# A scratch write on GpSimd between the gathers of a graph convolution

## The chip, the core and the metric

The kernel runs on one core of one Trainium2 chip. The time is in device microseconds (us). PE is the matrix engine, DVE the vector engine, ACT the scalar engine, POOL is GpSimd, and SP is the engine that issues most plain transfers. "L614" is line 614 of the kernel before.

## The reference, cut to what matters

A graph has N = 6250 nodes with D = 128 features and E = 200000 edges, sorted by destination. After a layer norm and a ReLU, two convolutions and one attention layer follow.

```
def mesh_conv(x, src, dst, ea, w1, b1, g, bt, w2, b2):
    m = concatenate([x[dst], x[src], ea]) @ w1 + b1        # one row for each edge
    m = silu(group_norm(m, g, bt)) @ w2 + b2
    return segment_sum(m, dst) / clip(count(dst), 1)       # mean over a node's edges

h = mesh_conv(h, ...); h = silu(group_norm(h)) + t_emb_term
h = mesh_conv(h, ...); h = silu(group_norm(h)) + h0
o = softmax attention over each node's edges, projected, normed
out = x + h + o
```

The change lies in the two convolutions alone.

## The kernel before, in words

For each convolution a node stage first multiplies all nodes by the two halves of `w1`. The half for destinations goes to DRAM as three bf16 pieces (`a3_d`), the half for sources as fp32 (`b_d`, 512 bytes a node). Then the edges run through in 196 chunks of CH = 1024 edges (NT = 8 groups of 128).

For one chunk, `ahead` does four things. `loads` fetches over SP's queue the relative destinations (`rel_b`), the edge attributes (`ohT`) and a window of destination rows (`pk`); DVE makes a one-hot matrix of `rel_b` (L454). `gather` issues eight indirect DMAs on POOL (L459), each fetching 128 source rows of `b_d` into the chunk's buffer `g`. `hidden` lets PE multiply the one-hot matrix by the window (L578, 24 products of 128x128) into PSUM `m`.

`first` adds `m` to the gathered rows (L590, DVE), squares them (L592, ACT) and sums them for the variances (L593). After a run of up to eight chunks `deviations` makes the factors, and `second` finishes one chunk: three DVE passes over `g` (L604, L607, L608), silu (L609, ACT), a one-hot matrix of destinations (L465), the product that sums the edges of a node (L614, PE, into `u`), two masked copies (L648, ACT) and an addition into the table (L639, DVE).

`pipeline` writes this order out: at step n `ahead(n+1)`, then `first(n)`, then `second` of a chunk some eight older. There are G + 5 = 13 buffers `g`, used in turn, so the gathers of chunk c must wait for L614 of chunk c-13.

The order in which each engine's instructions stand in the program is settled when it is built: instructions of one engine are placed by a scheduler that looks at their dependencies and at when it expects the engine to be free, not by the order of the Python lines alone. Each engine then works through its own list in that order. Behind the 196 chunks stands a loop for edges that fit no window (`leftovers`), which all engines enter and leave together. After the second convolution comes attention, with gathers of `kv_d`.

Of the kernel before, what the change touches and what calls it, by code (L numbers as in the profile page):

```python
# [8 lines left out]
FP = mybir.dt.float32  # L9
# [10 lines left out]
P = 128  # L20
# [2 lines left out]
HD = 16  # L23
NT = 8
CH = NT * P
G = 8
WN = 112
KE = P - WN
# [9 lines left out]
def kernel(ctx: ExitStack, tc: tile.TileContext, x, src, dst, eat, w, out):  # L38
# [10 lines left out]
    nc = tc.nc  # L49
# [392 lines left out]
    def loads(c, pools, rows_d):  # L442
        k = Chunk()
        k.c = c
        k.src, k.dm = src_i[:, c * NT:(c + 1) * NT], dm0[:, c * NT:(c + 1) * NT]
        k.rel = pools["rel"].tile([WN, CH], BF, name="rel_b")
        nc.sync.dma_start(
            out=k.rel, in_=rel_d[c * NT:(c + 1) * NT, :].rearrange("t p -> (t p)")[None, :].to_broadcast([WN, CH]))
        k.ohT = pools["ohT"].tile([P, CH], BF, name="ohT")
        nc.sync.dma_start(out=k.ohT[WN:P, :], in_=ea_d[:, c * CH:(c + 1) * CH])  # L450
        k.pk = pk[c % NPK]
        first = value(lo_i, c, SP, N - 1)
        nc.sync.dma_start(out=k.pk[:WN].rearrange("p s c -> p (s c)"), in_=rows_d[bass.ds(first, WN), :])
        nc.vector.tensor_scalar(k.ohT[:WN, :], k.rel, iota_p[:WN], None, ALU.is_equal)  # L454
        return k

    def gather(k, g, table_d):
        for t in range(NT):
            nc.gpsimd.indirect_dma_start(  # L459
                out=g[:, t, :table_d.shape[1]], out_offset=None, in_=table_d,  # L460
                in_offset=bass.IndirectOffsetOnAxis(ap=k.src[:, t:t + 1], axis=0))
# [7 lines left out]
    def leftovers(body, pools):  # L469
# [5 lines left out]
        with tc.For_i(0, nout, 1) as c:  # L475
# [3 lines left out]
            with tc.For_i(0, n, 1) as r:  # L479
# [13 lines left out]
                k.win = nc.s_assert_within(at + r, 0, NW - 1, skip_runtime_bounds_check_because=WHY)  # L493
                k.ea = lp.tile([KE, CH], BF, name="l_ea")
                nc.sync.dma_start(out=k.ea, in_=ea_d[:, bass.ds(c * CH, CH)])
                body(k)
# [17 lines left out]
    def spread(n):  # L514

        sizes = [G] * max(0, (n - 5) // G)
        rest = n - sum(sizes)
        while rest:
            s = min(max(rest // 2, 1), G)
            sizes.append(s)  # L520
# [26 lines left out]
    def conv(i):  # L547
# [4 lines left out]
        with ExitStack() as es:  # L552
# [3 lines left out]
            gp, wk, vp = pool("gp", 1), pool("wk", 2), pool("vp", 2)  # L556
            ps_ = pools["ps"]

            gs = [gp.tile([P, NT, PITCH], FP, name=f"g{j}") for j in range(G + 5)]
            if i == 1:  # L560
# [11 lines left out]
            def hidden(k, terms):  # L572
                k.m = ps_.tile([P, NT, D], FP, name="m", tag="m", bufs=2)
                for t in range(NT):
                    e = slice(t * P, (t + 1) * P)
                    pairs = [(lhs[:, e], rhs[:, s, :]) for lhs, rhs in terms for s in range(3)]
                    for j, (a, b) in enumerate(pairs):
                        nc.tensor.matmul(k.m[:, t, :], lhsT=a, rhs=b, start=(j == 0), stop=(j == len(pairs) - 1))  # L578

            def ahead(c):  # L580
                k = loads(c, pools, a3_d[i])
                k.g = gs[c % len(gs)]
                gather(k, k.g, b_d[i])
                hidden(k, [(k.ohT, k.pk)])
                return k

            def first(k, var, j):

                k.mt = k.g[:, :, :D]
                nc.vector.tensor_tensor(k.mt, k.m, k.mt, ALU.add)  # L590
                sq = wk.tile([P, NT, D], FP, name="sq")
                nc.scalar.activation(sq, k.mt, AF.Square)  # L592
                return lambda: nc.vector.tensor_reduce(  # L593
                    var[:, j * NT * H:(j + 1) * NT * H], sq.rearrange("p t (g c) -> p (t g) c", c=HD), AX.X, ALU.add)

            def deviations(n, var):
                sd = vp.tile([P, G * NT * H], FP, name="sd")
                nc.scalar.activation(sd[:, :n], var[:, :n], AF.Sqrt, bias=eps_t, scale=1.0 / HD)
                rs = ps_.tile([P, G * NT * H], FP, name="rs")
                nc.vector.reciprocal(rs[:, :n], sd[:, :n])  # L600
                return rs
# [17 lines left out]
            def first_step(k):  # L619
                for f in state["reduce"]:  # L620
                    f()
                if state["j"] == 0:
                    state["var"] = vp.tile([P, G * NT * H], FP, name="var")
                state["reduce"] = [first(k, state["var"], state["j"])]
# [17 lines left out]
            def second(k):  # L642
# [7 lines left out]
                state["late"].append(k)  # L650

            pipeline(ahead, first_step, between, second, add_late)

            wcl = pools["left"].tile([KE, 3, D], BF, name="wcl")
# [17 lines left out]
    def after_conv(i, A):  # L672
# [15 lines left out]
        nc.scalar.activation(A[:, :NW, :], A[:, :NW, :], AF.Silu)  # L688

    conv(1)  # L690
    with tc.tile_pool(name="node1", bufs=1) as np_:
        A = np_.tile([P, NW + 1, D], FP, name="A")
        after_conv(1, A)
        nc.vector.tensor_tensor(A[:, :NW, :], A[:, :NW, :], temb[:, None, :].to_broadcast([P, NW, D]), ALU.add)
        make_ab(A, 2)
    conv(2)
    with tc.tile_pool(name="node2", bufs=1) as np_:
        A = np_.tile([P, NW + 1, D], FP, name="A")
# [25 lines left out]
    with ExitStack() as es:  # L724
# [3 lines left out]
        gp, wk = pool("gp", G + 3), pool("wk", 2)  # L728
# [271 lines left out]
```

## Time and profile before

| | |
|---|---|
| median of 3 runs | 8192.53 us (8170.84 to 8251.86) |
| profiled execution | 8242.21 us, span 8240.4 us |
| mean granted PE clock | 0.666 |
| POOL busy | 4542.3 us (55%), 4723 instructions |
| DVE busy | 5153.9 us (63%) |
| PE busy | 3684.0 us (45%) |
| ACT busy | 1631.0 us (20%) |
| gathers of the convolutions (L459) | 3136 of 949 ns |
| first gather of the first, second convolution | 213.17 us, 2888.77 us |

Busy time is the sum of an engine's rows. A row of the timeline gives start, duration, engine, line, operation, what it writes and reads, how often, and in brackets how long the engine had been idle and what ended that. A row of the waits gives who waited for whom, the sum in us, the number of times and the longest. A row of the windows gives a stretch, its length, then busy time and number of instructions of PE, the weight loads, DVE, ACT and POOL, then the clock, the share of time in which the DMA engines were busy and GB/s. "remote" stands for a wait whose releaser the profile does not show, "issue" for time in which the engine waited for nothing that it shows.

### The profile page before, as it was taken

Reading aid. Unit: us, or ns where it says so; the run is one execution under the profiler, and the core shown is the slowest. Engines: PE = TensorE matmul, PEld = TensorE weight load, DVE = VectorE, ACT = ScalarE, POOL = GpSimd, SP = SyncE. Lnnn points to the kernel's source line nnn. Section 1 sums busy time; section 2 is a strip of 40 time slices with the busy share of each in tenths; the row PEclk is TensorE's granted clock in tenths of the full one; section 3 lists DMA queues with packets and bytes.
Section 4 is the critical chain, followed back from the end, with each engine's and each line's share of the span. In section 5 each row is a group of like instructions: output and inputs, shape, how many; then the busy total and the mean of one; then the engine's idle time right before and its main releaser. Section 6 shows DMA issues by size and latency. Waiting matters only on the chain. (4 is left out here: it accounts for less than half of the span.)

```text
span 8240.4 us, 87011 instructions
## 1 busy us (share of the span) xinstructions
PE 3684.0 (45%) x26465; PEld 3255.2 (40%) x26466; DVE 5153.9 (63%) x7719; ACT 1631.0 (20%) x3110; POOL 4542.3 (55%) x4723
## 2 busy tenths in 40 slices
PE   2144444444444414444444444442555555555553
PEld 1133343334334313433334433332444545544542
DVE  5266666666666726666666666683666666666666
ACT  2122222222222312222222222230000000000001
POOL 2556566666565056656656665504666666666650
PEclk9566666666666656666666666676676666666666
DMA  5222222222222122222222222213444444444441
GB/s 160 63 70 71 69 74 73 71 72 73 68 70 65 43 61 73 70 68 72 72 70 71 73 73 69 65 71 111 118 120 120 120 120 120 120 120 118 120 110 48
DMA packets 422049, 702.81 MB, mean 85 GB/s; under 512 B 116780, under 2 KB 237444, under 8 KB 421060
## 3 DMA queue, kind: packets, MB, share of 16 engines
q0 software_dynamic: 175616, 417.77, 18.7%
q1 hardware_dynamic: 210920, 258.43, 10.3%
q10 hardware_dynamic: 35036, 20.95, 0.9%
q8 instruction: 215, 3.52, 0.2%
q14 instruction: 262, 2.15, 0.1%
HBM read 649.99 MB, written 46.67 MB: 85 GB/s over the span
## 5 line engine op out<-in xcount | busy, mean ns | idle before, releaser
L459 POOL DMA_INDIRECT g<-b_d,src_i x3136 | 2977.0, 949 | 2227.8 <-PE u L614 785.5
L459 POOL DMA_INDIRECT g<-kv_d,src_i x1568 | 1523.4, 972 | 1164.6 <-issue 418.7
L614 PE MATMUL u<-g,oh 128*128 128x129 f32 (+1 forms) x6272 | 1292.0, 380 | 1309.6 <-ACT g L609 659.9
L614 PEld LDWEIGHTS u<-g,oh 128*128 128x128 f32 x6272 | 1183.8, 286 | 1418.7 <-ACT g L609 710.8
L578 PE MATMUL m<-pk,ohT 128*128 128x128 bf16 x9408 | 894.5, 258 | 1609.9 <-issue 977.8
L578 PEld LDWEIGHTS <-ohT 128*128 128x128 bf16 x9408 | 744.8, 118 | 1742.4 <-issue 1170.7
L639 DVE TENSOR_TENSOR flat<-flat,u 128x258 f32 (+1 forms) x392 | 164.2, 419 | 1343.2 <-ACT u L648 1178.1
L828 PE MATMUL u<-g,oh 128*128 128x145 f32 x3136 | 785.8, 438 | 420.6 <-issue 361.7
L828 PEld LDWEIGHTS u<-g,oh 128*128 128x128 f32 x3136 | 723.7, 318 | 454.8 <-issue 391.0
L648 ACT ACTIVATE u<-u,mask 128x129 f32<-128x129 f32 (+1 forms) x784 | 266.5, 340 | 2152.5 <-remote 1250.7
L590 DVE TENSOR_TENSOR g<-m,g 128x1024 f32<-128x1024 f32 x392 | 476.2, 1215 | 290.8 <-remote 232.8
L740 PE MATMUL qe<-pk,ohT 128*128 128x128 bf16 x4704 | 439.1, 257 | 367.0 <-DVE g L752 226.3
L609 ACT ACTIVATE g<-g 128x1024 f32<-128x1024 f32 x392 | 414.1, 1056 | 925.8 <-DVE g L608 471.4
L592 ACT ACTIVATE sq<-g 128x1024 f32<-128x1024 f32 x392 | 414.3, 1057 | 718.6 <-DVE g L590 438.7
L740 PEld LDWEIGHTS <-ohT 128*128 128x128 bf16 x4704 | 382.4, 119 | 406.1 <-issue 204.2
L872 DVE SCALAR_TENSOR_TENSOR nm<-u,nm 128x2 f32<-128x2 f32 x196 | 31.2, 159 | 768.1 <-remote 467.6
L454 DVE TENSOR_SCALAR ohT<-rel_b,iota_p 112x1024 bf16<-112x1024 bf16 x588 | 299.1, 514 | 331.6 <-remote 313.4
L593 DVE TENSOR_REDUCE var<-sq 128x64 f32<-128x1024 f32 x392 | 473.8, 1209 | 15.5 <-ACT sq L592 13.7
L465 DVE TENSOR_TENSOR oh<-cps,dm 128x1024 f32<-128x1024 f32 x392 | 476.7, 1216 | 0.0
L607 DVE TENSOR_TENSOR g<-g,cps 128x1024 f32<-128x1024 f32 x392 | 475.1, 1212 | 1.8
L608 DVE TENSOR_TENSOR g<-g,cps 128x1024 f32<-128x1024 f32 x392 | 475.2, 1212 | 0.2
L604 DVE TENSOR_TENSOR g<-g,rs 128x1024 f32<-128x1024 f32 x392 | 473.8, 1209 | 0.1
(196 smaller groups left out, 3563.9 us busy)
## 6 DMA issues: line engine op xcount, KB each, us to landing
rel_b<-rel_d SPq DMA_DIRECT2D x588, 224.0 KB
g<-b_d,src_i POOLq DMA_INDIRECT x3136
pk<-a_d SPq DMA_DIRECT2D x588, 84.0 KB
g<-kv_d,src_i POOLq DMA_INDIRECT x1568
ohT<-ea_d SPq DMA_DIRECT2D x588, 32.0 KB
a_d<-a SPq DMA_DIRECT2D x48, 192.0 KB
kv_d<-kv ACTq DMA_DIRECT2D x49, 132.0 KB
h_d<-A SPq DMA_DIRECT2D x2, 3136.0 KB
```

Of the source, the lines that this page charges most:

```text
L459: nc.gpsimd.indirect_dma_start(out=g[:, t, :table_d.shape[1]], out_offset=None, in_=table_d, in_offset=bass.IndirectOffsetOnAxis(ap=k.src[ ...
L465: nc.vector.tensor_tensor(k.oh, iota[:, None, :].to_broadcast([P, NT, P]), k.dm[:, :, None].to_broadcast([P, NT, P]), ALU.is_equal)
L578: nc.tensor.matmul(k.m[:, t, :], lhsT=a, rhs=b, start=(j == 0), stop=(j == len(pairs) - 1))
L590: nc.vector.tensor_tensor(k.mt, k.m, k.mt, ALU.add)
L592: nc.scalar.activation(sq, k.mt, AF.Square)
L593: return lambda: nc.vector.tensor_reduce(var[:, j * NT * H:(j + 1) * NT * H], sq.rearrange("p t (g c) -> p (t g) c", c=HD), AX.X, ALU.add)
L604: nc.vector.tensor_tensor(k.mt.rearrange("p t (g c) -> p t g c", c=HD), k.mt.rearrange("p t (g c) -> p t g c", c=HD), k.rs.rearrange("p (t ...
L607: nc.vector.tensor_tensor(k.mt, k.mt, over_edges(gam), ALU.mult)
L608: nc.vector.tensor_tensor(k.mt, k.mt, over_edges(bet), ALU.add)
L614: nc.tensor.matmul(k.u[:, 0, :wide], lhsT=k.oh[:, t, :], rhs=k.g[:, t, :wide], start=(t == 0), stop=(t == NT - 1))
L740: nc.tensor.matmul(qe[:, t, :], lhsT=lhs[:, e], rhs=rhs[:, s, :], start=(s == 0), stop=(s == 2))
L828: nc.tensor.matmul(k.u[:, :wide], lhsT=k.oh[:, t, :], rhs=k.g[:, t, :wide], start=(t == 0), stop=(t == NT - 1))
```

## The change

A constant REST = 1280 is added. In each convolution a scratch tile `rest` of 128 x 1280 fp32 is taken from the pool `wk` with one buffer, and `ahead` writes zeros to it with a memset on GpSimd, in the Python code behind the eight gathers of the chunk. Nothing reads the tile.

```
+REST = 1280
...
+            rest = wk.tile([P, REST], FP, name="rest", bufs=1)
+
             def ahead(c):
                 k = loads(c, pools, a3_d[i])
                 k.g = gs[c % len(gs)]
                 gather(k, k.g, b_d[i])
+                nc.gpsimd.memset(rest, 0.0)
                 hidden(k, [(k.ohT, k.pk)])
                 return k
```

The chunks of `leftovers` and the attention layer do not use it. There are 2 x 196 = 392 such memsets. In the changed program they differ from each other in no way that the scheduler would see: each writes the same tile, waits for the memset before it, and is awaited by no other engine.

More of the change, by code (lines that the diff above doesn't have):

```diff
@@ L25 @@
 CH = NT * P
+REST = 1280
 G = 8
@@ L578, in hidden @@
                         nc.tensor.matmul(k.m[:, t, :], lhsT=a, rhs=b, start=(j == 0), stop=(j == len(pairs) - 1))
+            rest = wk.tile([P, REST], FP, name="rest", bufs=1)
             def ahead(c):
@@ L583, in ahead @@
                 gather(k, k.g, b_d[i])
+                nc.gpsimd.memset(rest, 0.0)
                 hidden(k, [(k.ohT, k.pk)])
```

## The prediction

> **What bounds the kernel now.** I read the page first (engines, costliest groups), then POOL's waits, then windows over single stretches, then the timeline where stages meet. The trace is of one core at a mean granted clock of 0.666.
>
> ```profile
> PE 3684.0 (45%) x26465; PEld 3255.2 (40%) x26466; DVE 5153.9 (63%) x7719; ACT 1631.0 (20%) x3110; POOL 4542.3 (55%) x4723
> ...
> L459 POOL DMA_INDIRECT g<-b_d,src_i x3136 | 2977.0, 949 | 2227.8 <-PE u L614 785.5
> ```
>
> No engine is full. POOL's row understates it: a gather shows as 949 ns, but on the timeline the next one starts 1.25 us after the last. A chunk's eight gathers so cost POOL 10.0 us, and the 392 chunks of the convolutions follow each other at 12.56 us (the additions of L590, chunk 20 to chunk 188 of the first convolution: 2110 us over 168). POOL is 80% taken in the loops and has 2.5 us to spare per chunk.
>
> ```profile
> ACT u L648 <- remote: 1250.7, 137, 22.7
> ...
> POOL g L459 <- PE u L614: 785.5, 288, 55.1
> ```
>
> POOL's spare time is waiting for a free gather buffer: chunk c takes the buffer of chunk c-13, free when its L614 product is done. So compute sets the pace. What holds compute is in the other line: ACT waits 1250.7 us in L648 for a mark that no row explains. One case:
>
> ```profile
> 2031.08 2.02 PE L614 MATMUL u<-g,oh 128*128 128x129 f32 x16 [2.37 <-issue]
> ...
> 2036.22 0.95 POOL L459 DMA_INDIRECT g<-b_d,src_i  x1 [0.30 <-issue]
> ...
> 2039.15 0.94 POOL L459 DMA_INDIRECT g<-b_d,src_i  x1 [1.98 <-remote]
> 2039.21 0.72 ACT L648 ACTIVATE u<-u,mask 128x129 f32<-128x129 f32 x2 [8.28 <-remote]
> ```
>
> PE's product ends at 2033.1 by its row; ACT, which needs it, starts at 2039.21, about when POOL's train of gathers pauses for 1.98 us. This repeats along the loop: while gathers run back to back, PE's completions reach the others late. Keep this for the third rival.
>
> How far the gathers run ahead of use decides what a later gather costs:
>
> ```profile
> 837.62 0.94 POOL L459 DMA_INDIRECT g<-b_d,src_i  x1 [0.59 <-remote]
> ...
> 871.55 1.21 DVE L590 TENSOR_TENSOR g<-m,g 128x1024 f32<-128x1024 f32 x1
> ...
> 3309.99 0.94 POOL L459 DMA_INDIRECT g<-b_d,src_i  x1 [0.30 <-issue]
> ...
> 3342.43 1.21 DVE L590 TENSOR_TENSOR g<-m,g 128x1024 f32<-128x1024 f32 x1
> ```
>
> The first pair is chunk 48 of the first convolution (last gather, then its first use), the second is chunk 32 of the second: 33.0 and 31.5 us from the end of gathering to use. Chunk 0's data came 1.6 us after its last gather (223.23 to 224.87), so the slack is 31.4 and 29.9 us.
>
> **What the Trainium skill says.** "GPSIMD Engine Reference", section "Engine selection", puts one-input work on GpSimd at about line rate; with the clock and width of its section "Specifications" (1.2 GHz, eight cores of 16 fp32) 1280 columns are an estimated 1.07 us. "Perfetto Trace Analysis", section "GPSIMD Engine Instruction", says to time such instructions by start-to-start spacing, not by their rows; the gathers agree (1.25 against 0.949 us). "SBUF — State Buffer", section "Who interferes with whom", says a VectorE instruction with two SBUF inputs contends only with a GpSimd one that reads SBUF. The scratch write reads nothing, so I charge DVE nothing; no line of this trace shows it.
>
> **The change part by part.** It adds 392 memsets of 128x1280 fp32 on POOL and nothing else; apart from a few neighbours exchanged on DVE, ACT and SP, costed at nothing, the other engines keep their order. But the memset depends only on the memset before it, and the built order does not put one behind each chunk. First convolution: 70 ahead of the first gather, 1 ahead of chunk 13, 125 in groups (mostly 3 or 4, every eighth chunk 10 or 11) from chunk 15 to ahead of chunk 48, none later. Second: 129 ahead of the first gather, 2 ahead of chunk 13, 65 up to ahead of chunk 32. So it is four lumps, not a rest per chunk.
>
> Price of one:
>
> ```profile
> 0.28 0.10 POOL L986 MEMSET const-float32-0.0<- 128x1 f32 x1
> ...
> 0.76 0.20 POOL masks.py:197 MEMSET ident<- 128x128 f32 x1 [0.29 <-POOLq L986]
> ```
>
> One column takes 100 ns and 128 take 205 (groups view), 0.83 ns per column: 1.16 us for 1280. Each memset also waits on POOL's own mark of the one before; POOL wakes 0.08 us after ACT's marks (a cast ends at 108.94, ea_f starts at 109.02). I take 1.25 us; the bounds are 1.16 (wait free) and 1.5 (the 0.30 us that lies between gathers).
>
> Lump 1. The first memset waits for the last ea_b cast and its store (issued at 129.90), so it starts near 132; 70 x 1.25 = 87.5 ends at 220. The cover is POOL's 84.83 us of idle time:
>
> ```profile
> 213.17 1.30 POOL L459 DMA_INDIRECT g<-b_d,src_i  x1 [84.83 <-DVE g L562]
> ...
> 2740.86 0.20 DVE L676 TENSOR_SCALAR icnt<-flat 128x49 f32<-128x49 f32 x1 [2.31 <-issue]
> ...
> 2888.77 0.94 POOL L459 DMA_INDIRECT g<-b_d,src_i  x1 [238.78 <-SPq L435]
> ```
>
> It runs out 7 us too early, and chunk 0's use follows its gather by 1.6 us, so all 7 us count.
>
> Lump 3. The 129 stand behind the loop that closes the first convolution, which all engines leave together; DVE's first instruction after it is at 2740.86. 129 x 1.25 = 161 ends at 2902, 13 us behind the old first gather. (The 238.78 us of idle time are no cover as a whole: 90 of them lie before the loop's end.)
>
> Lumps 2 and 4, in the loops:
>
> ```profile
> 393.00:839.00 446.00, 190.88 (x1415) 167.75 (x1413) 279.50 (x286) 110.09 (x154) 273.84 (x288) 0.67 0.24 69
> 3073.00:3311.00 238.00, 111.75 (x792) 97.65 (x792) 157.35 (x160) 60.59 (x85) 151.75 (x160) 0.66 0.25 71
> ```
>
> These windows are chunks 13 to 48 and 13 to 32; the last bracket before the clock counts the gathers. 288 x 1.25 = 360 of 446 us: 86 spare. The lump is 125 x 1.25 = 156, so chunk 48's data come 70 us later; 31 are slack, 39 reach DVE at L590. In the second 160 x 1.25 = 200 of 238: 38 spare, 81 added, 43 late, 30 slack, 13 reach DVE. Behind the waiting L590 stand, in DVE's order, the second pass of older chunks and with it the release of the buffers.
>
> After each lump the lead is gone and must be rebuilt by gathers back to back, the situation of the 2039 case. Its harsh form is the start: in the 131 us of chunks 0 to 12 only three L590 finish before the train ends at 343. Rebuilding three chunks of lead should cost less; bounds 0 (it rebuilds in waits that exist anyway) and 33 us (compute stands still meanwhile). I take 16 each.
>
> Sum: 7 + 39 + 13 + 13 + 2 x 16 = 104 us. On the profiled execution (8242.2, span 8240.4) that gives 8346; that run lies 0.6% above the median of the three timed ones, 8192.5, and on their scale it is about 8297.
>
> **The rivals.**
> - Mostly hidden: the lumps lie in waits, memsets cost 1.16 us, rebuilding is free. Lumps 1 and 3 then give 0 and 2, the loops 28 and 7: about 37, or less where a relieved PE gives some back. For it: 785.5 us of buffer waits. Against: the spare per stretch is counted above. Time 8220.
> - Dearer memset, 1.5 us: lumps 24, 70, 46 and 30, with rebuilding 202; time 8395. For it: the 0.30 us between gathers. Against: the bare memsets at the start follow each other in 0.03 us.
> - Faster: the pauses let PE's marks through. Place: L648, 1250.7 us over 392 chunks, 3.2 us each; over the 55 chunks of lumps 2 and 4 at most 176. But POOL's own work in chunks 13 to 48 must fit 446 + 31 us for the gain to arrive, so it decides only if a memset costs POOL under about (477 - 360) / 125 = 0.94 us, and for most of the gain under 0.7. A half to two thirds of the 176 gives 8085. Against: both memset rows and the skill's rate.
> - A rest behind every chunk, as the diff reads, would lie in each chunk's 2.5 us and relieve all 392. The built order rules it out.
>
> **How the numbers follow.** Forecast 0.55 (own range 8240 to 8350), hidden 0.20, dearer 0.15, faster 0.10. A measurement tells about 1% (82 us) from no change. Of the forecast some three quarters lie over 1%: 0.42, with the dear case 0.57 slower. Hidden, the rest of the forecast and a little of the faster case make 0.35 within 1%; 0.08 faster. The range of 8200 to 8400 leaves out the faster case and the dear one's upper half.
>
> **What would show it.** Right: 392 memset rows near 1.16 us, none after about 900 us in the first convolution; the first gathers near 220 and 2910; between chunks 30 and 48 ACT's L592 or DVE's L590 waiting for gathers; POOL's waits for PE u L614 smaller. Wrong: memsets starting under 1.0 us or over 1.5 us apart, L590 of chunk 48 no later than 871 plus lump 1's shift, or L648's wait for remote falling by hundreds of microseconds with no gather late.

## The result, and the profile after

The changed kernel takes 8293.42 us (median of 9 runs, 8281.94 to 8308.44); the kernel before, run beside it, 8191.32 us (9 runs, 8151.82 to 8251.86). The ratio is 1.0138, with a 95% interval from 1.0117 to 1.0158: 96 to 129 us more. The forecast was 8297 us, 104 us more. In the kernel after, the lines around the change stand one to four lower: L459 is L460, L590 is L594, L592 is L596, L614 is L618, L648 is L652; the memset is L587.

The page of the kernel after, first the engines, then the costliest groups (busy us, mean ns, idle time before and what ended it), with the group of the memsets:

```profile
PE 3679.1 (44%) x26465; PEld 3273.2 (39%) x26466; DVE 5169.5 (62%) x7719; ACT 1631.3 (20%) x3110; POOL 4998.1 (60%) x5115
...
L460 POOL DMA_INDIRECT g<-b_d,src_i x3136 | 2971.2, 947 | 1730.0 <-issue 742.0
...
L594 DVE TENSOR_TENSOR g<-m,g 128x1024 f32<-128x1024 f32 x392 | 476.3, 1215 | 506.1 <-DMA g<-b_d,src_i 259.3
...
L587 POOL MEMSET rest<- 128x1280 f32 x392 | 463.5, 1182 | 109.8 <-DVEq L476 85.9
```

POOL has 392 more instructions and 456 us more of busy time; the other engines execute as many instructions as before. What is new is in the third line: the additions now wait 259.3 us for gathers. In the kernel before, the waits view has 14.6 us for that pair.

The memsets also slow some of DVE's work. The addition L594 takes 1215 ns in both kernels, but DVE's busy time is 15.6 us higher, and 10.4 of them are in the one-hot matrix L454. Its source view in the kernel before, after, and in the one with memsets of double length that comes below (durations min/median/max in ns):

```profile
L454 DVE TENSOR_SCALAR ohT<-rel_b,iota_p x588: 468/480/714, 190.9 to 8071.8; 112x1024 bf16<-112x1024 bf16 x196
```

```profile
L455 DVE TENSOR_SCALAR ohT<-rel_b,iota_p x588: 467/481/1460, 190.4 to 8118.4; 112x1024 bf16<-112x1024 bf16 x196
```

```profile
L455 DVE TENSOR_SCALAR ohT<-rel_b,iota_p x588: 466/481/2549, 191.5 to 8299.2; 112x1024 bf16<-112x1024 bf16 x196
```

In the changed kernel the 23 of these rows that overlap a memset take 0.95 us on average, the other 565 take 0.51 and none of them over 0.73. That is 10 us of DVE's time in all. Whether any of it reaches the end of the kernel, no run separates.

The lead of a chunk is the time from the end of its gathers to the start of its use, the addition. The timeline of the kernel after, at the places that the prediction named (start, duration, engine, line, operation; in brackets the idle time before it):

```profile
131.26 3.61 POOL L587 MEMSET rest<- 128x1280 f32 x3 [4.12 <-DMA ea_d<-ea_b]
...
220.77 1.30 POOL L460 DMA_INDIRECT g<-b_d,src_i  x1 [0.19 <-DMA ohT<-ea_d]
...
907.89 0.94 POOL L460 DMA_INDIRECT g<-b_d,src_i  x1 [0.30 <-remote]
...
910.49 1.22 DVE L594 TENSOR_TENSOR g<-m,g 128x1024 f32<-128x1024 f32 x1 [6.25 <-DMA g<-b_d,src_i]
...
2801.21 1.17 POOL L587 MEMSET rest<- 128x1280 f32 x1 [85.95 <-DVEq L476]
...
2959.75 0.95 POOL L460 DMA_INDIRECT g<-b_d,src_i  x1 [0.15 <-issue]
...
3412.95 0.94 POOL L460 DMA_INDIRECT g<-b_d,src_i  x1 [0.30 <-DMA g<-b_d,src_i]
...
3415.65 1.22 DVE L594 TENSOR_TENSOR g<-m,g 128x1024 f32<-128x1024 f32 x1 [6.32 <-DMA g<-b_d,src_i]
```

The fourth line is the use of chunk 48 of the first convolution, the last that of chunk 32 of the second; the gather above each is that chunk's last. Before, 33.0 and 31.5 us lay between the end of that gather and its use. Now 1.7 and 1.8 us do (908.84 to 910.49, 3413.89 to 3415.65), and the addition names the gather as what it waited for: the lead is gone. Chunk 48's use has moved from 871.55 to 910.49, by 38.9 us. Seven chunks on, when the lead is back at 31 us, the shift is 55.4 us.

A warning about the two profiles: from one to the other the spans differ by 48 us only, against 102 us between the medians. The attention stage, which the change doesn't touch, is 24 us shorter in the trace after. Over all the traces of this study, its length is either 2785 to 2798 us or 2815 to 2822, for kernels whose source is the same there. The profiled execution of the kernel before lies 51 us above the median of its runs beside it. Nor is a convolution free of it: in the kernel below that has memsets in the second convolution alone, the unchanged first one is 37.9 us longer than before, and its chunk 20 is used 10.3 us later. A lead is read within one trace and is firm. A shift of 10 or 20 us between two traces is firm only where several pairs of traces show it, and a total of a few tens of microseconds isn't.

### The profile page after: what moved, and what is told of

Its sections match the earlier page's. It is cut to its first block, busy times and chain, and to the rows that moved or that the text cites. A ratio compares the mean times of both kernels' runs of the same rounds, so it can differ in the third digit from the quotient of the medians.

```text
span 8288.4 us, 87405 instructions
## 1 busy us (share of the span) xinstructions
PE 3679.1 (44%) x26465; PEld 3273.2 (39%) x26466; DVE 5169.5 (62%) x7719; ACT 1631.3 (20%) x3110; POOL 4998.1 (60%) x5115
## 5 line engine op out<-in xcount | busy, mean ns | idle before, releaser
L460 POOL DMA_INDIRECT g<-b_d,src_i x3136 | 2971.2, 947 | 1730.0 <-issue 742.0
L460 POOL DMA_INDIRECT g<-kv_d,src_i x1568 | 1520.9, 970 | 1144.3 <-issue 417.9
L618 PE MATMUL u<-g,oh 128*128 128x129 f32 (+1 forms) x6272 | 1299.4, 384 | 1234.9 <-ACT g L613 792.3
L618 PEld LDWEIGHTS u<-g,oh 128*128 128x128 f32 x6272 | 1196.0, 290 | 1348.3 <-ACT g L613 867.2
L594 DVE TENSOR_TENSOR g<-m,g 128x1024 f32<-128x1024 f32 x392 | 476.3, 1215 | 506.1 <-DMA g<-b_d,src_i 259.3
L652 ACT ACTIVATE u<-u,mask 128x129 f32<-128x129 f32 (+1 forms) x784 | 266.5, 340 | 1997.3 <-remote 1209.4
L596 ACT ACTIVATE sq<-g 128x1024 f32<-128x1024 f32 x392 | 414.2, 1057 | 920.7 <-DVE g L594 527.5
L587 POOL MEMSET rest<- 128x1280 f32 x392 | 463.5, 1182 | 109.8 <-DVEq L476 85.9
L466 DVE TENSOR_TENSOR oh<-cps,dm 128x1024 f32<-128x1024 f32 x392 | 476.3, 1215 | 0.0
```

What stands on the lines that cost most here:

```text
L460: nc.gpsimd.indirect_dma_start(out=g[:, t, :table_d.shape[1]], out_offset=None, in_=table_d, in_offset=bass.IndirectOffsetOnAxis(ap=k.src[ ...
L466: nc.vector.tensor_tensor(k.oh, iota[:, None, :].to_broadcast([P, NT, P]), k.dm[:, :, None].to_broadcast([P, NT, P]), ALU.is_equal)
L587: nc.gpsimd.memset(rest, 0.0)
L618: nc.tensor.matmul(k.u[:, 0, :wide], lhsT=k.oh[:, t, :], rhs=k.g[:, t, :wide], start=(t == 0), stop=(t == NT - 1))
```

## The experiments

All ratios are to the kernel before, timed beside it on the same chip.

**One convolution at a time.** The memset stays in one of the two, in the same places.

```
-                nc.gpsimd.memset(rest, 0.0)
+                if i == 1:
+                    nc.gpsimd.memset(rest, 0.0)
```

> Memsets in the first convolution alone (70 ahead of its first gather, 126 between chunks 13 and 48). Theory (POOL's time counts only beyond its spare time and the lead of the gathers): lump 1 late by 7.6 us, 39 us at chunk 48, 16 us to rebuild the lead, together +62 us, ratio 1.0076. Rival (the memsets cost POOL's time in full, or what is lost is made up by the end of the loop): +240 us or about 0.

Measured: 1.0085 [1.0065, 1.0104], some 70 us. The theory's 62 us lies in the interval, both rivals lie far outside. In its trace the first gather is 9.1 us later, the lead is 1.6 to 3.7 us in chunks 32 to 48, and the use of chunk 48 is 40.8 us later, that of chunk 55 66.9. The whole first convolution is 103.2 us longer in this trace and 61.7 in that of the full change, with the same memsets in the same places: so wide is the scatter of single traces.

The other one has `if i == 2`.

> Memsets in the second convolution alone (129 ahead of its first gather, 67 between chunks 13 and 32). The sum of the prediction gives +42 us (13 + 13 + 16), ratio 1.0051; the two traces differ by only 11 us there, ratio 1.0013. The first: the two single traces hide part of it in their scatter. The second: lumps 3 and 4 were priced too high, and the 102 us between the medians are not made of these four lumps alone.

Measured: 1.0066 [1.0042, 1.0090], some 54 us. The second convolution is 26.3 us longer in this trace, and in the trace of the full change 10.6 us. The timed ratio is in accord with the prediction's 42 us and not with 10.6, which is within the scatter of single traces. The two ratios add up to 1.5%, the whole change to 1.4% [1.2, 1.6].

**The lumps at the starts alone.** 70 and 129 memsets stand ahead of the two loops; the 193 inside the loops are left out.

```
+            for _ in range(70 if i == 1 else 129):
+                nc.gpsimd.memset(rest, 0.0)
...
-                nc.gpsimd.memset(rest, 0.0)
```

> 70 and 129 memsets ahead of the first gather of each convolution and none in the loops (199 in all; the other 193 are left out). Theory: only the overhang of the covers counts, 7.6 + 9.3 = +17 us, ratio 1.0021. Rival (memsets on POOL slow the node stages beside them, where DVE, ACT and PE work): +40 us or more, and the first gather of the second convolution more than 20 us later than the lump's end explains.

Measured: 1.0019 [1.0000, 1.0038], some 16 us. In its trace the first gathers are 6.6 us later in the first convolution and 9.2 us in the second (28.1 less the 18.9 by which the first had ended later), and the lead in the loops is 26 to 45 us (chunks 20 to 120), as in the kernel before. So some 1.2 of the 1.4% come from the lumps inside the loops. The theory's 17 us fit and the rival's 40 don't; the interval, 0 to 31 us, can't tell whether both starts count or the first alone.

**A pause that does stand between all chunks.** Instead of the scratch tile the memset clears the chunk's own buffer ahead of its gathers, so the order is forced: a pause per chunk. The length is 1024 columns.

```
                 k.g = gs[c % len(gs)]
+                nc.gpsimd.memset(k.g[:, :, :D], 0.0)
                 gather(k, k.g, b_d[i])
```

> One memset of 128x1024 columns per chunk, about 1.0 us, written into the chunk's own gather buffer ahead of its eight gathers, so that it can't move: what the diff seems to say (the gathers overwrite it). Theory of POOL's load alone: 10.0 + 1.0 us fit into the 12.5 us per chunk, within 0.5% of before. Rival (pauses in the train of gathers let the marks of PE through): ACT's wait in L648 for remote falls from 1250 us by a third or more and the kernel is 2 to 5% faster. Third (the memset stands behind the release of the buffer and makes the gathers later, lead down by 1 us): slower by under 0.5%.

Measured: 1.0058 [1.0043, 1.0074], some 48 us slower, where the two expectations without a gain had 0.5% at most. The waits view of this kernel (who waits for whom, us in total, times, longest), then POOL's groups from its page; here the memset is L583, and what stands behind it is one line lower than before, so L648 is L649:

```profile
ACT u L649 <- remote: 1711.5, 176, 27.8
...
L459 POOL DMA_INDIRECT g<-b_d,src_i x3136 | 2975.8, 949 | 948.1 <-issue 831.4 <-POOL g L583 92.0 <-PE u L615 14.6
...
L583 POOL MEMSET g<- 128x1024 f32 x392 | 376.3, 962 | 953.3 <-remote 330.5 <-DMA a_d<-a 321.9 <-PE u L615 287.0
```

The wait that a pause per chunk was to shorten (1250.7 us at ACT's masked copies before) grew to 1711.5 us, with the lead still at 26 to 33 us in the loop. So a rest with every chunk is no gain in this form, and the third rival falls in it. But it is more than a rest: the memset must wait for the release of the buffer (287.0 us for L615) and the gathers for the memset (92.0 us), and the one-hot matrices L454 take 31 us more of DVE. Why the wait grew is not settled by any run here.

**Half and double the length.** With REST = 640 and 2560, the scheduler puts more or fewer of the memsets ahead of the loops.

```
-REST = 1280
+REST = 640
```

> The scratch tile has 640 columns instead of 1280, so a memset is half as long: 0.83 ns a column and 0.10 us give a row of 0.63 us, 0.69 us from start to start (the measured 1.222 less half of 1280 columns). The built order puts 129 of them ahead of the first convolution's first gather, 67 into chunks 13 to 24, and all 196 of the second ahead of its first gather. Theory (spare time and lead are thresholds): the start is later by some 8 us (129 x 0.69 = 89 from 131.3 on); the 67 in the loop are 46 us against 11 chunks x 2.5 = 28 us of spare time, so gathers fall 18 us behind, which the lead of 31 us takes up, and the use of chunks 24 and 48 is later by the start's shift alone; in the second convolution 196 x 0.69 = 135 us end before the gather that the kernel before issues 150 us after the loop's end, so nothing. Sum 8 us: ratio 1.001. Rival (each memset costs in proportion to POOL's time, wherever it stands): 0.69/1.222 of 1.38% = 0.8%: ratio 1.008. Rival (half a pause per gather train lets PE's marks through and a cheap one gains): under 0.998.

> The scratch tile has 2560 columns, so a row of 2.23 us and 2.28 us from start to start. The built order puts 37 ahead of the first convolution's first gather and 158 into its chunks 15 to 96, 67 ahead of the second's first gather and 128 into its chunks 14 to 81. Theory (thresholds): start +3 us; 158 x 2.28 = 360 us against 83 chunks x 2.5 = 208 of spare time, 152 behind, 31 taken up by the lead, 121 reach DVE, and 16 for rebuilding the lead: 140 us. Second: start +5 us; 128 x 2.28 = 292 against 68 x 2.5 = 170, 122 behind, 30 taken up, 92 and 16: 113 us. Sum 253 us: ratio 1.031, with the lead of the gathers at about 2 us from some chunk near 30 to chunk 96 of the first convolution. Rival (in proportion to POOL's time): 2.28/1.222 of 1.38% = 2.6%: ratio 1.026. Rival (what is lost is only the rebuilding of the lead and the starts, once per convolution, however long the lump): no more than the change itself, 1.014.

Measured: half 1.0022 [1.0009, 1.0035], some 18 us; double 1.0371 [1.0348, 1.0394], some 303 us. A cost in proportion to POOL's time (0.8 and 2.6%) is out on both sides, too high for the half and too low for the double. The cost grows faster than the time that the memsets take, as with a threshold. The tile view of the scratch tile in the two kernels (durations min/median/max in ns) and, of the double one, chunk 96 on the timeline:

```profile
L587 POOL MEMSET rest<- x392: 631/631/3790, 129.9 to 2879.2; 128x640 f32 x196
```

```profile
L587 POOL MEMSET rest<- x392: 2232/2232/5391, 131.5 to 4171.3; 128x2560 f32 x196
...
1592.91 0.95 POOL L460 DMA_INDIRECT g<-b_d,src_i  x1 [0.30 <-PE u L618]
...
1595.57 1.22 DVE L594 TENSOR_TENSOR g<-m,g 128x1024 f32<-128x1024 f32 x1 [4.69 <-DMA g<-b_d,src_i]
```

In the double kernel the lead is between 1.6 and 8 us from chunk 20 to chunk 96 (1.7 us in the lines shown), and the use of chunk 96 is 136.4 us later. The first convolution ends 144.7 us later (140 expected), the second is 105.6 us longer (113 expected). The 250 us of the traces lie below the 303 us timed; the profiled execution before, from which they are counted, is itself 61 us above the median of the runs beside this kernel, so the 50 us need no further mechanism, but no run places them.

The half kernel told something the theory had not said. It expected the lead to hold, as the gathers fall behind by only 18 us. But the lead is down to 1.7 us at chunk 20. Left out the later start (9.9 us), that chunk's gathers end 13 us later than before, and it is used 18.9 us sooner: the larger part of the lead goes because compute is early. Then, when the lead is back at 27 us at chunk 26, the use is 6.1 us later than before on the same count.

This early compute is no scatter. From the use of chunk 12 to that of chunk 20, the seven convolutions with memsets among these chunks (in the full change, each part alone, half and double) take 79 to 87 us. The seven without, with 13 buffers, take 99 to 110. ACT's idle time ahead of its masked copies in that stretch is 18 to 33 us in the first seven and 47 to 55 in the others. With a memset ahead of every chunk it is 98 to 109 us, with 45 to 55 of idle time. The two uses in DVE's timeline, before and after:

```profile
417.81 1.22 DVE L590 TENSOR_TENSOR g<-m,g 128x1024 f32<-128x1024 f32 x1
...
518.37 1.21 DVE L590 TENSOR_TENSOR g<-m,g 128x1024 f32<-128x1024 f32 x1
```

```profile
425.44 1.23 DVE L594 TENSOR_TENSOR g<-m,g 128x1024 f32<-128x1024 f32 x1
...
504.98 1.22 DVE L594 TENSOR_TENSOR g<-m,g 128x1024 f32<-128x1024 f32 x1 [4.28 <-PE m L579]
```

The windows view over the same 150 us of the kernels before and after (stretch, length, busy time and instructions of PE, weight loads, DVE, ACT, POOL, then clock, DMA share, GB/s):

```profile
393.00:543.00 150.00, 63.34 (x471) 55.60 (x469) 93.21 (x97) 36.45 (x53) 97.48 (x103) 0.68 0.24 69
```

```profile
393.00:543.00 150.00, 70.73 (x554) 65.18 (x554) 111.79 (x112) 42.49 (x58) 116.24 (x115) 0.73 0.23 64
```

PE and DVE do more in the second, 554 instead of 471 products and 112 instead of 97 instructions, though the kernel had started later. The waits view over this stretch has ACT's wait for a releaser that the profile doesn't show, before and then after:

```profile
ACT u L648 <- remote: 54.4, 6, 15.0
```

```profile
ACT u L652 <- remote: 5.6, 1, 5.6
```

This one line varies: over the same 150 us it is 31.8 and 58.5 us in the two kernels without memsets there (the starts alone, the second convolution alone), and 8.9 and 36.0 in two with them (half, double). The sum over ACT's waits above is the safer figure. So, while the lead lasts, the lump has the effect that the third rival claimed: compute runs 14 to 22 us ahead. That it does so because PE's completions reach ACT in time is not shown; that fewer gathers are under way meanwhile would do as well, and no run separates the two. What was gained has to be given back: in the half kernel the use loses 25 us from chunk 20 to 26, while the lead returns.

**Fewer buffers.** If restoring a lead costs that much, so does building it at the start. The kernel before, without memsets, with 12, 11, 10 and 9 gather buffers in place of 13. The scheduler's order on other engines changes somewhat with it, so this is not one edit alone.

```
-            gs = [gp.tile([P, NT, PITCH], FP, name=f"g{j}") for j in range(G + 5)]
+            gs = [gp.tile([P, NT, PITCH], FP, name=f"g{j}") for j in range(G + 3)]
```

> The kernel before with 12 gather buffers instead of 13 and no memset. The planner's order on PE, DVE and SP changes somewhat with it. While the lead of the gathers was used up in chunks 13 to 20, the kernel with the memsets and the one with half of them ran 19 to 21 us ahead of the kernel before, start's shift left out, and building the lead up again cost 16 to 19 us. If this is what a chunk of lead costs (it is bought by gathers back to back, during which PE's marks come late), one buffer less saves the purchase of some 12 of 31 us of lead, some 7 us in each convolution, and nothing is lost as long as 18 us of lead cover the unevenness of compute: ratio 0.998. Rival: the lead covers the bursts of the second passes (the longest waits for a buffer are 50 us), and with one chunk less POOL stands idle and DVE waits at L590: ratio over 1.005. The wait of POOL for L614 should grow in both; the wait of DVE at L590 for gathers tells them apart (under 50 us in the first, hundreds in the second).

> As the one with 12 buffers, with 11: the lead falls by 25 of 31 us. First theory: 14 us saved in each convolution, ratio 0.997, if 6 us of lead still cover the unevenness. Rival: late gathers at L590 in most groups of eight chunks; the additions of a group wait for the last second pass of the group before it: ratio 1.02 or more, growing from 12 to 11 buffers.

> As before with 10 gather buffers. With 12 and 11 the use of chunk 12 came 10.7 and 20.2 us earlier in the first convolution (the first train of gathers is one and two chunks shorter), with 1.0 and 2.0 tenths of a per cent a convolution measured, and the lead in the loop fell from some 33 to 24 and 12 us. First theory: the start gains another 10 us, but the lead is then near zero, so DVE waits for gathers at L590 in most chunks: about 1.00, the turning point. Rival (late gathers cost nothing as long as POOL's 10.0 us fit the 12.56 us of a chunk): another 0.2%: ratio 0.994.

> As before with 9 gather buffers, one more than the run of eight chunks that second passes work off, so no lead at all: the gathers of a chunk start when the L614 of the chunk nine before is done. First theory: every chunk's use waits for its own gathers, ten microseconds behind the release of a buffer, and the additions of a group slip against the second passes: ratio over 1.03. Rival (POOL's time fits): 0.992.

| buffers | ratio | lead in chunks 20 to 120, us (median) | chunk 12's use in the first convolution, us |
|---|---|---|---|
| 13 | 1 | 26 to 45 (34) | 0 |
| 12 | 0.9985 [0.9968, 1.0003] | 14 to 29 (20) | -10.7 |
| 11 | 0.9961 [0.9943, 0.9979] | 2 to 19 (9) | -20.2 |
| 10 | 1.0116 [1.0087, 1.0144] | 2 to 10 (2) | -19.2 |
| 9 | 1.0486 [1.0456, 1.0516] | 92 to 114 (105) | 52.8 |

With 9 buffers the gathers of a chunk stand in the program ahead of the second pass of the chunk whose buffer they take, so part of the data is overwritten. They don't wait for that pass, and the lead is 105 us instead of the none that was expected: this kernel says nothing of a short lead, though its ratio is over the 1.03 of the first theory. With 12 buffers no difference is shown. With 11, the kernel is 0.4% faster than the one before and so faster than both. The additions at the start of the first convolution, in the timeline of DVE, before and with 11 buffers:

```profile
345.77 1.22 DVE L590 TENSOR_TENSOR g<-m,g 128x1024 f32<-128x1024 f32 x1
359.91 1.22 DVE L590 TENSOR_TENSOR g<-m,g 128x1024 f32<-128x1024 f32 x1
```

```profile
334.91 1.22 DVE L590 TENSOR_TENSOR g<-m,g 128x1024 f32<-128x1024 f32 x1
339.38 1.22 DVE L590 TENSOR_TENSOR g<-m,g 128x1024 f32<-128x1024 f32 x1
343.86 1.22 DVE L590 TENSOR_TENSOR g<-m,g 128x1024 f32<-128x1024 f32 x1
347.78 1.22 DVE L590 TENSOR_TENSOR g<-m,g 128x1024 f32<-128x1024 f32 x1
```

With a first train two chunks shorter the additions start sooner. Both convolutions gain about 20 us at chunk 12 (20.2 and 21.1), of which the timing keeps 32 [17, 47] in all. With 10 buffers the same start is gained, and lost in the loop, as the waits view of that kernel shows against 14.6 us before and 25.1 us with 11:

```profile
ACT sq L592 <- DVE g L590: 941.3, 130, 88.9
DVE g L590 <- DMA g<-b_d,src_i: 904.1, 207, 7.8
```

So a lead of about 9 us nearly covers the unevenness of compute, and 33 are more than the loop needs, as far as kernels show it that differ in the scheduler's order too. The expectation for 10 buffers, a wash, was too low by 1%.

## Why the prediction was right, step by step

**Where the memsets stand.** As read from the built order: none runs in the first convolution after chunk 48's gathers, nor in the second after chunk 32's (the last starts at 3402.9).

**The price of one.** 1.25 us was taken; the first 70 start 1.222 us apart, with a row of 1.165 us. The rows of 631, 1165 and 2232 ns for 640, 1280 and 2560 columns are 0.834 ns a column and 0.10 us: the two small memsets at the program's start had given that to two digits. The estimate of 1.07 us from the Trainium skill's "GPSIMD Engine Reference", section "Engine selection", was 8% short. What the prediction put too high is the wait for the mark (the completion signal) of the one before: 0.057 us, not 0.085. A dearer memset (1.5 us) is out, as is a cheap one.

**DVE charged nothing.** This step failed, though it is small: 10 us of DVE's time in the one-hot matrices, as shown above. The prediction's reason spoke of VectorE instructions with two SBUF inputs. Those that ran longer beside a memset are TENSOR_SCALAR operations, which read one large tile.

**Lump 1.** 7 us predicted; 7.6 in this trace, 9.1 and 6.6 in the two others with the same lump. That it came so near is luck: two errors cancel. At the measured price the 70 memsets would take 85.5 us and make the gather 3.8 us late. They took 89.3, because one of them took 4.32 us instead of 1.165 and four more followed 0.16 us late. The long one, at 155.71, runs beside a DVE pass of the node stage. That pass in the kernel before, then the memset's row (three in one) and the pass in the kernel after:

```profile
156.01 3.43 DVE L428 TENSOR_SCALAR A<-A 128x6272 f32<-128x6272 f32 x1
```

```profile
153.26 6.77 POOL L587 MEMSET rest<- 128x1280 f32 x3
154.80 4.13 DVE L429 TENSOR_SCALAR A<-A 128x6272 f32<-128x6272 f32 x1
```

Both are longer: the pass takes 4.13 us instead of 3.43, and the three memsets 6.77 where three alone take 3.61. With memsets of half and double length one memset is longer by the same 3.16 us there. So the node stage beside the lump is not free of it.

**Lump 2.** With lump 1, 46 us at chunk 48 were predicted, and 38.9 came (40.8 with the first convolution alone). Chunk 48's gathers ended 70.3 us later rather than 77. Half of the difference is the memset's price (125 x 0.028 = 3.5 us), the rest that POOL had somewhat more time to spare than 86 us. The slack, 31 us, is what was used up (70.3 less 38.9).

**Lump 3.** 13 us predicted at the first gather; 9.3, 9.3 and 9.2 us in three traces, the difference being the price again. But the step that failed is the next: that all of it reaches compute. At chunk 12 of the second convolution, only 1.3, 1.6 and 2.3 us are left of it (the shift of the use, less the shift with which the convolution began), so some 11 of the 13 us of this term don't arrive. In the first convolution the start's delay stays whole (7.6 us at chunk 12). In the second it is there in the uses of chunks 0 and 1 (9.4 and 16.6 us later), turns over in chunk 2 (32.1 us sooner) and is 1.1 us from chunk 4 on, much the same in all three traces: it is taken up while the first train of gathers runs. Which wait of the train does it was not tried.

**Lump 4.** 13 us predicted; chunk 32 comes 10.2 us later, counted from chunk 12, and 10.3 in the kernel that changes this convolution alone.

**Rebuilding the lead.** Taken at 16 us from bounds of 0 and 33, the least certain term. Chunks 48 to 55 of the first convolution show 16.5 us (26.1 with that convolution alone), chunks 32 to 55 of the second 6.9 us (21.4 with that one alone). Read at chunk 48 instead, the second gives 21.1 and 36.3: the term is of the order predicted, and the traces don't fix it closer. The reason given, that gathers back to back hold compute up, fits the half kernel, where the use loses 25 us while the lead returns; as a cause it is argued. That the same lead had been worth 20 us while it was being spent was not in the sum; it didn't have to be, because at chunk 48 the gathers alone set the time, wherever compute had been in between.

**The sum.** By the traces, term by term, the first convolution comes to 55 us at chunk 55 (62 predicted) and the second to 18 us, or 33 in the kernel that changes it alone (42 predicted): 73 to 88 us, for which the sum was too high. Timed, the full change costs 113 us [96, 129], for which it was too low. Single traces with a scatter of some 40 us in a convolution can't settle the difference. That 104 fell so near is in part chance: lump 1 was right by two errors, lump 3 failed by 11 us, and rebuilding was a guess between bounds. The single parts as timed, 70 and 54 us against 62 and 42, have the prediction inside their intervals.

**The rivals.** Mostly hidden (8220) falls with the lead of 1.7 us at chunk 48 and with a timed cost of at least 96 us. The faster case was given its condition rightly: POOL's work must fit the stretch. At 1.222 us a memset it doesn't. Its effect is nevertheless there, in chunks 13 to 20, while the prediction weighed it only as a whole over 55 chunks. Of the signs named, POOL's wait for L614 fell (785.5 to 675.8 us), and L648's wait for "remote" did not fall by hundreds (1250.7 to 1209.4 us):

```profile
ACT u L652 <- remote: 1209.4, 124, 20.5
...
POOL g L460 <- PE u L618: 675.8, 308, 49.3
```

## What to carry to other kernels

An instruction that nothing waits for is not placed where the source has it: look at the built order, and price it as the lumps it forms. Each lump costs its length less the engine's spare time over its own stretch, less the lead of the buffers, and then the price of restoring that lead. Below this threshold it costs little (here half the length cost a sixth), above it the whole excess. An instruction on GpSimd can also lengthen one on DVE beside it, and be lengthened by it: compare the longest rows, not the medians. More buffers than the lead needs are not free either: here 11 beat 13 by 0.4%, and 10 lost 1.2%.

## What had not been expected of the hardware

A GpSimd memset of fp32 takes 0.834 ns a column from 640 to 2560 columns and leaves 0.057 us to the next one that waits for it. Beside such memsets DVE's one-hot operation took up to 1.46 us (1280 columns) and 2.55 us (2560 columns) where rows without one beside them stayed under 0.73, and one memset took 4.32 us instead of 1.165 beside a DVE pass over 128x6272, while the addition stayed at 1.22 us. With memsets among the gathers of chunks 13 to 20, ACT idled 18 to 33 us there ahead of its masked copies instead of 47 to 55; with a memset ahead of every chunk's gathers its wait over the whole kernel rose from 1250.7 to 1711.5 us. And the untouched attention stage has two lengths, some 20 us or more apart, from one execution to the next.
